# The column table of a graph layer turned during set-up, and 174 instead of 144 chunks taken from it

## The chip, the cores and the metric

The kernel runs on one core of one Trainium2 chip. The metric is the device time of one execution in microseconds; a profiled execution gives a span (first to last instruction) as well. Engines are called PE (matmul; its weight loads are PEld), DVE, ACT, POOL and SP, as in the profile.

## The reference, cut to what matters

There are 12500 nodes with 128 features and 200000 edges that are sorted by destination. Each node's normalised row is sent along its edges, the incoming rows are averaged, and a network of four layers with a residual ends it.

```python
h = jnp.maximum(_layernorm(x, axis=-1), 0.0)
# _L0_gnn_ref(z=h, edge_index=(src, dst)):
msgs = z[src]
agg = jax.ops.segment_sum(msgs, dst, num_segments=n)
deg = jax.ops.segment_sum(jnp.ones((src.shape[0],), z.dtype), dst, num_segments=n)
agg = agg / jnp.maximum(deg, 1.0)[:, None]
h = jax.nn.relu(agg @ Wg + z @ Ws + bg)
h = jnp.tanh(h @ W1 + b1)
h = jnp.tanh(h @ W2 + b2)
x = x + (h @ W3 + b3)
```

## The kernel before

**Chunks.** The edges are cut into 1563 chunks of 128. For each chunk the 128 source rows must stand in SBUF with one edge on each partition; PE then multiplies them with a one-hot matrix (`oh`, made by DVE for groups of 8 chunks, in 5 buffers) and adds the result into the sums of a block of up to 512 nodes, in PSUM (`agg`, and `edge` for chunks that lie across two blocks). Chunks are added in their order.

**Three sources of rows.** (1) 1339 chunks are gathered by POOL with one indirect DMA each from `htab`, the table of normalised rows in DRAM (tile `rows`, line 451 before). A gather writes into one of `AHEAD = 26` buffers, so POOL runs at most 26 gathers ahead of PE. (2) 80 chunks (10 groups of 8, "raw") are gathered from `x` during set-up, before `htab` exists; DVE normalises them later, group by group, in the main loop's first part (lines 266 to 280 on tile `raw`). (3) 144 chunks come from `tab`, the same table turned and kept in SBUF, with a node in each column. An edge's column is copied from `tab` at an index that a register holds. ACT makes 72 of these chunks (`column_copies`) and DVE 72 (`column_pairs`). One instruction handles two edges, so a chunk is 64 instructions, in 8 blocks with a register load (`TENSOR_LOAD places`) ahead of each. Then PE turns the finished 128x128 tile (`cols`) and ACT copies it to `turned`, which is used like `rows`. `SHARES` holds the two counts, `FROM` the first chunk that may be taken this way, `ENDS` the last for ACT and for DVE.

**Order.** PE, ACT, SP and the columns on DVE run in the order in which the code is written; the rest of DVE and the set-up are ordered by a scheduler. The main loop walks over the chunks and counts gathered chunks (`behind`). The column instructions of a chunk are written so that they end `MARGIN = 28` gathers before its use on ACT and 36 on DVE; the turn on PE is written 14 gathers before its use. ACT has 4 buffers of columns, DVE 6. The network's layers are spread between the chunks; from chunk `QUICK = 1312` a planner places them by its own reckoning of when each gather lands.

**Set-up.** The nodes are read in 11 pieces (of up to 10 tiles of 128 nodes). DVE and ACT normalise a piece into `h` (2 buffers), and SP writes it to `htab`. `indices` turns the edge lists on PE. POOL spends this time on the 80 raw gathers. In the main loop's first 48 chunks `own` reloads the rows of `htab` by SP in 25 pieces (`xb`, 256 KB each), and `own_turned` turns them on PE and copies them on ACT into `tab`. The columns wait for the whole of `tab`.

Of the kernel before, what the change touches and what calls it, by code (L numbers as in the profile page):

```python
# [22 lines left out]
F32 = mybir.dt.float32  # L23
# [8 lines left out]
P = 128  # L32
EPS = 1e-5
CPR = 16
BLK = 512
# [10 lines left out]
BEHIND = 2  # L46
EVERY = 4
AT = 3
SHARES = 72, 72
FROM, ENDS = 80, (1480, 1540)  # L50
MARGIN = 28
SUMS_AT, BANK = 1 << 25, 2048
AHEAD_OF_USE = 2
# [27 lines left out]
def windowed(ctx, tc, x, src, dst, Wg, Ws, bg, W1, b1, W2, b2, W3, b3, out, flag):  # L81
    nc = tc.nc
    N, D = x.shape
# [48 lines left out]
    for c in slots:  # L132
        shares = [n / k * (c < end) for n, k, end in zip(SHARES, within, ENDS)]
        owed = [o + n for o, n in zip(owed, [*shares, 1 - sum(shares)])]
# [6 lines left out]
    blocks, n = [], 0  # L141
# [46 lines left out]
    ps_m = ctx.enter_context(tc.tile_pool(name="ps_m", bufs=4, space=PSUM))  # L188
# [5 lines left out]
    for t, a in ((rsrc, src), (rdst, dst)):  # L194
        a = a[RAW0 * P : RAW1 * P].rearrange("(u e) -> u e", u=NRAW)[:, : GRP * P]
# [18 lines left out]
    for g in range(NRAW):  # L214
        t = raws.tile([P, GRP, D], F32, name=f"raw{g}")
# [7 lines left out]
    ident = const.tile([P, P], F32, name="ident")  # L223
# [14 lines left out]
    htab = dram.tile([NP, D], F32, name="htab")  # L238
    bytes_at = dram.tile([ahead_of + NROW * ROW + past_end], U8, name="bytes_at")
    tab = const.tile([P, NP], F32, name="tab")  # L240
# [24 lines left out]
    def centre(pool, xt, k, stats, bufs=2):  # L265
        nc.vector.tensor_reduce(stats[:, 0], xt, AX.X, ALU.add)
        nc.vector.scalar_tensor_tensor(xt, spread(stats[:, 0], k), -1.0 / D, xt, op0=ALU.mult, op1=ALU.add)  # L267
        sq = (pool.tile([P, PIECE, D], F32, name="sq") if bufs > 1 else pool.tile([P, GRP, W_RAW], F32, name="ohr", bufs=1)[:, :, :D])[:, :k]
        if bufs > 1:
            nc.scalar.activation(sq, xt, AF.Square)  # L270
        else:
            nc.vector.tensor_tensor(sq, xt, xt, op=ALU.mult)
        nc.vector.tensor_reduce(stats[:, 1], sq, AX.X, ALU.add)

    def factors(stats):
        nc.scalar.activation(stats[:, 1], stats[:, 1], AF.Sqrt, bias=eps, scale=1.0 / D)
        nc.vector.reciprocal(stats[:, 1], stats[:, 1])

    def scale(h, xt, k, stats):
        nc.vector.scalar_tensor_tensor(h, xt, 0.0, spread(stats[:, 1], k), op0=ALU.max, op1=ALU.mult)  # L280

    with tc.tile_pool(name="ln", bufs=2) as ln:
# [80 lines left out]
        for i, (t0, k) in enumerate(pieces):  # L363
            xt = ln.tile([P, PIECE, D], F32, name="xt", bufs=3)
            whole = min(N - t0 * P, k * P) // P
            rest = min(N - t0 * P, k * P) - whole * P
            if rest:
                nc.vector.memset(xt[:, whole, :], 0.0)
            nc.sync.dma_start(xt[:, :whole, :], x[t0 * P : (t0 + whole) * P, :].rearrange("(t p) d -> p t d", p=P))
            if rest:  # L370
                nc.sync.dma_start(xt[:rest, whole, :], x[(t0 + whole) * P : N, :])
            if i == 1:
                indices("src", src, 0, keep_src)
            stats = ps_a.tile([P, BLK], F32, name="agg")[:, : 2 * k].rearrange("p (s t) -> p s t", s=2)
            xt = xt[:, :k]
            centre(ln, xt, k, stats)
            factors(stats)
            h = ln.tile([P, PIECE, D], F32, name="h", bufs=2)
            scale(h[:, :k], xt, k, stats)
            nc.sync.dma_start(htab[t0 * P : (t0 + k) * P, :].rearrange("(t p) d -> p t d", p=P), h[:, :k])  # L380


        number = sp.tile([NROW, CPR], F32, name="number")
# [50 lines left out]
    ml = ctx.enter_context(tc.tile_pool(name="ml", bufs=2))  # L434
# [11 lines left out]
    def sp_dma(*a):  # L446
        tc.keep_in_program_order(nc.sync.dma_start(*a))
# [87 lines left out]
    def onehot(g):  # L535
        k = min(GRP, NCH - g * GRP)
        is_raw = raw(g * GRP)
        w = W_RAW if is_raw else W
        oh = ed.tile([P, GRP, W_RAW], F32, name="ohr", bufs=1) if is_raw else oh_bufs[g % OHS]
        newest[:] = [nc.vector.tensor_tensor(  # L540
            oh[:, :k, :w], lane[:, None, :w].to_broadcast([P, k, w]),
            dloc[:, g * GRP : g * GRP + k][:, :, None].to_broadcast([P, k, w]), op=ALU.is_equal,
        )]
        for c in range(g * GRP, g * GRP + k):
            if c in lanes[0] or c in lanes[1]:
                r, q = divmod(c, CPR)
                nc.vector.scalar_tensor_tensor(
                    oh[:, c % GRP, :W], lane[:, :W], partner[:, r, q // EVERY : q // EVERY + 1], oh[:, c % GRP, :W],
                    op0=ALU.is_equal, op1=ALU.subtract,
                )  # L550
        ohs[g] = oh
# [189 lines left out]
                s = out  # L741
            nc.vector.tensor_tensor(out, s, rd[:, a0 - n : a1 - n], op=ALU.mult)

    owns, xss, stores = {}, {}, []

    def own(s):

        n0 = s * BLK
        k = -(-min(BLK, N - n0) // P)
        hb = ml.tile([P, BLK // P, D], F32, name="xb")  # L750
        sp_dma(hb[:, :k], htab[n0 : n0 + k * P, :].rearrange("(t p) d -> p t d", p=P))
        owns[s] = hb

    def own_turned(s):

        k = -(-min(BLK, N - s * BLK) // P)
        hb = owns.pop(s)
        pt = ps_m.tile([P, BLK // P, P], F32, name="pm")
        for t in range(k):
            pe.transpose(pt[:, t, :], hb[:, t, :], ident)  # L760
        act.copy(tab[:, s * BLK : s * BLK + k * P], pt[:, :k, :].rearrange("p t n -> p (t n)"))

    def own_part(b):

# [155 lines left out]
            if w[1] is None:  # L920
                work.remove(w)

    nown = -(-N // BLK)
    own(0)
    own(1)
    own_turned(0)
    own(2)
    onehot(0)
    onehot(1)
    told_begins()  # L930
# [3 lines left out]
    for c in range(NCH):  # L934
        g = c // GRP
        at = c
        store(c - (SOON if c >= QUICK else LATE))
        if c % GRP == 0 and g + 2 < ngrp:
            onehot(g + 2)
            if raw((g + 2) * GRP):  # L940
                raw_scaled(((g + 2) * GRP - RAW0) // STEP)
            if g == 2 + NRAW + 2:
                worst = checked()
            if 2 <= g < 2 + NRAW:
                centre(ed, raw_rows[g - 2], GRP, raw_stats(g - 2), bufs=1)
            if g == 2 + NRAW + 5:
                factors(stats_raw)

        if c % (GRP // 2) == 0 and g + 2 < ngrp:
            copies, times = loading[1]  # L950
            while times and times[0] <= behind:
                times.pop(0)
                next(copies, 0)
        while c % GRP == GRP // 2 and counted < len(blocks) and reach[counted][-1] // GRP <= g + (c >= QUICK):
            count(counted)
            counted += 1
        while nxt < len(order) and nxt < behind + AHEAD:
            gather(order[nxt])
            nxt += 1
        if not raw(c) and c not in apart:  # L960
            behind += 1
            copies, times = loading[0]
            while times and times[0] <= behind:
                times.pop(0)
                next(copies, 0)
            while turns and turns[0][0] <= behind:
                turn(turns.pop(0)[1])
        if c >= QUICK:

            there = 7.5 + 1.251 * (NRAW * GRP + order.index(c)) if c not in apart else 0  # L970
            if c == QUICK:
                now = there - SPREAD
            while soonest() and max(now, soonest()[2]) < there:
                go_on(soonest())
            now = max(now, there) + 0.27
        add(c)

        lead = LEAD if c < QUICK else 2
        if done < len(blocks) and (c - lead if across[done] else c) >= reach[done][-1]:
            quick = reach[done][-1] + LEAD >= QUICK  # L980

            prev, older = (i if i >= 0 and reach[i][-1] + LEAD < QUICK else None for i in (done - 1, done - 2))
            older = None if quick and prev is None else older
            work.append([layers(done, prev, older), 0, 0, 0, quick and blocks[done][1] <= P])
            done += 1

        if c % TILE_EVERY == 1 and c // TILE_EVERY < NT:
            tallied(c // TILE_EVERY)
            if c // TILE_EVERY == NT - 1:
                outside(worst)  # L990
            if c // TILE_EVERY + EARLY < NT:
                seen(c // TILE_EVERY + EARLY)
        if c % 2 == 1 and c // 2 + 1 < nown:
            own_turned(c // 2 + 1)
            if c // 2 + 3 < nown:
                own(c // 2 + 3)
        if c < QUICK:
            if c % 2 == 0:
                go_on(work[0] if work else None)
                fetch_ahead(c)  # L1000
        if c == QUICK:
            for b, (_, n) in enumerate(blocks):
                if n < BLK:
                    own_part(b)
# [376 lines left out]
```

## Time and profile before

| | |
|---|---|
| runs | 1799.81, 1805.12, 1805.02 us; median 1805.02 |
| the profiled execution | 1800.16 us, with a span of 1798.4 us |
| busy PE / DVE / ACT / POOL | 1399.2 / 1034.4 / 1534.3 / 1348.5 us |
| mean granted PE clock | 0.83 |
| gathers of rows | 1339, the first issued at 107.3 us and the last at 1781.8 us |

Time is read from the engine that never waits for another: the share of busy time alone does not tell it, since an engine's gaps can be its own overhead. In the rows of a view, "x" is a count, and the text in brackets gives the idle time ahead of a row and what ended it. DVE, ACT and PE rows with a count are merged neighbours. [...]

### The profile page before, as it was taken

Reading aid. Unit: us, or ns where it says so; the run is one execution under the profiler, and the core shown is the slowest. Engines: PE = TensorE matmul, PEld = TensorE weight load, DVE = VectorE, ACT = ScalarE, POOL = GpSimd, SP = SyncE. Lnnn points to the kernel's source line nnn. Section 1 sums busy time; section 2 is a strip of 40 time slices with the busy share of each in tenths; the row PEclk is TensorE's granted clock in tenths of the full one; section 3 lists DMA queues with packets and bytes.
Section 4 is the critical chain, followed back from the end, with each engine's and each line's share of the span. In section 5 each row is a group of like instructions: output and inputs, shape, how many; then the busy total and the mean of one; then the engine's idle time right before and its main releaser. Section 6 shows DMA issues by size and latency. Waiting matters only on the chain.

```text
span 1798.4 us, 26668 instructions
## 1 busy us (share of the span) xinstructions
PE 1399.2 (78%) x5410; PEld 926.5 (52%) x5410; DVE 1034.4 (58%) x5580; ACT 1534.3 (85%) x5169; POOL 1348.5 (75%) x1428
## 2 busy tenths in 40 slices
PE   0047576878787888897888888787888888779998
PEld 0036454555455555555555555545555554555567
DVE  7965866666655656566565665556556655435400
ACT  1213999999999999999999999999999999998223
POOL 7777777777777777777777777777777777777774
PEclk9999999767887786877867868879787788778998
DMA  8954222222222222222222222222222222222221
GB/s 209 242 140 139 55 67 58 64 61 70 58 73 71 59 73 71 57 73 71 71 59 71 71 59 71 71 59 73 71 59 71 71 56 73 71 65 71 59 62 45
DMA packets 129832, 138.77 MB, mean 77 GB/s; under 512 B 30119, under 2 KB 106019, under 8 KB 129464
## 3 DMA queue, kind: packets, MB, share of 16 engines
q0 software_dynamic: 45408, 93.09, 19.9%
q1 hardware_dynamic: 80974, 40.37, 8.3%
q10 hardware_dynamic: 3276, 3.51, 0.7%
q14 instruction: 128, 1.05, 0.2%
q8 instruction: 46, 0.75, 0.2%
HBM read 123.84 MB, written 13.03 MB: 76 GB/s over the span
## 4 chain that ended last, share of the span: by engine, by line
ACT 29%; PE 25%; DMA 19%; issue 13%; POOL 9%; ACTq 4%; DVE 0%; DVEq 0%; POOLq 0%
ACT cols L518 25%; DMA rows<-htab,scol 19%; PE pm L441 17%; PE agg L441 6%; POOL rows L451 4%; POOL raw L217 4%; ACTq L461 4%; ACT h L518 3%; PE edge L441 2%; PE pm L444 1%; ACT turned L518 0%; ACT rd L521 0%; ACT o L521 0%; DVE cols L500 0%; DMA raw<-in_x_dram,rsrc 0%
## 5 line engine op out<-in xcount | busy, mean ns | idle before, releaser
L451 POOL DMA_INDIRECT rows<-htab,scol x1339 | 1267.8, 947 | 408.0 <-issue 226.7
L518 ACT ACTIVATE cols<-both_first,tab 128x2 f32<-128x2 f32 x4608 | 1351.2, 470 | 3.8 <-issue 1.9
L441 PE MATMUL pm<-h,w 128*128 128x512 f32 (+4 forms) x1344 | 795.0, 692 | 25.0 <-ACT h L518 20.5
L500 DVE SCALAR_TENSOR_TENSOR cols<-first_only,tab 128x2 f32<-128x2 f32 x4608 | 666.6, 218 | 250.4 <-issue 249.3
L441 PEld LDWEIGHTS agg<-oh,rows 128*128 128x128 f32 x1928 | 394.6, 253 | 426.8 <-DMA rows<-htab,scol 260.5
L441 PE MATMUL agg<-oh,rows 128*128 128x24 f32 x1928 | 398.7, 307 | 177.2 <-DMA rows<-htab,scol 172.2
L540 DVE TENSOR_TENSOR oh<-shared,dloc 128x192 f32<-128x192 f32 x186 | 65.5, 354 | 356.6 <-PE agg L441 211.0
L441 PEld LDWEIGHTS pm<-h,w 128*128 128x128 f32 x1344 | 243.6, 229 | 33.5 <-ACT h L518 22.4
L441 PEld LDWEIGHTS edge<-oh,rows 128*128 128x128 f32 x750 | 144.0, 233 | 164.8 <-DMA rows<-htab,scol 89.4
L441 PE MATMUL edge<-oh,rows 128*128 128x24 f32 x750 | 145.9, 289 | 63.3 <-DMA rows<-htab,scol 59.4
L518 ACT ACTIVATE h<-pm,b2c 128x512 f32<-128x512 f32 (+4 forms) x112 | 76.9, 689 | 51.6 <-PE pm L441 51.6
L217 POOL DMA_INDIRECT raw<-in_x_dram,rsrc x80 | 79.8, 998 | 25.6 <-issue 23.8
L587 DVE TENSOR_SCALAR_CACHE_REDUCE nearby<-nearby,parity 128x656 uint8<-128x656 uint8 x98 | 86.8, 886 | 0.0
L518 ACT ACTIVATE h<-pm,b1c 128x512 f32<-128x512 f32 (+4 forms) x112 | 76.6, 694 | 11.8 <-PE pm L441 11.2
L521 ACT COPY tab<-pm 128x512 f32<-128x512 f32 (+1 forms) x25 | 14.4, 577 | 68.1 <-PE pm L444 68.1
L340 PE MATMUL pm<-ident,idx_f 98*128 98x98 f32 x32 | 5.7, 373 | 82.5 <-DVE idx_f L334 54.4
L441 PEld LDWEIGHTS agg<-oh,turned 128*128 128x128 f32 x196 | 45.1, 258 | 36.6 <-issue 33.0
L444 PE MATMUL pm<-ident,cols 128*128 128x128 f32 x144 | 49.2, 342 | 10.7 <-ACT h L518 5.4
L518 ACT ACTIVATE turned<-pm 128x128 f32<-128x128 f32 x144 | 50.3, 349 | 7.4 <-PE pm L444 7.4
L740 DVE TENSOR_TENSOR mT<-agg,sums 128x136 f32<-128x136 f32 (+6 forms) x57 | 15.3, 272 | 71.3 <-PE agg L441 61.9
L441 PE MATMUL pm<-ident,h 128*128 128x128 f32 (+1 forms) x196 | 43.8, 309 | 14.4 <-ACT h L518 14.3
L270 ACT ACTIVATE sq<-xt 128x1280 f32<-128x1280 f32 (+3 forms) x11 | 12.7, 1153 | 44.6 <-DVE xt L267 35.4
(129 smaller groups left out, 850.8 us busy)
## 6 DMA issues: line engine op xcount, KB each, us to landing
rows<-htab,scol POOLq DMA_INDIRECT x1339
nearby<-bytes_at SPq DMA_DIRECT2D x98, 82.0 KB
xb<-htab SPq DMA_DIRECT2D x24, 256.0 KB
xb<-in_x_dram SPq DMA_DIRECT2D x23, 256.0 KB
out_dram<-o SPq DMA_DIRECT2D x23, 256.0 KB
xt<-in_x_dram SPq DMA_DIRECT2D x8, 640.0 KB
htab<-h SPq DMA_DIRECT2D x8, 640.0 KB
raw<-in_x_dram,rsrc POOLq DMA_INDIRECT x80
```

The lines of the kernel that those rows point to most:

```text
L217: nc.gpsimd.indirect_dma_start(out=t[:, j, :], out_offset=None, in_=x, in_offset=bass.IndirectOffsetOnAxis(ap=rsrc[:, g, j : j + 1], axis=0),)
L270: nc.scalar.activation(sq, xt, AF.Square)
L441: tc.keep_in_program_order(nc.tensor.matmul(*a, **k))
L444: tc.keep_in_program_order(nc.tensor.transpose(*a, **k))
L451: nc.gpsimd.indirect_dma_start(out=r, out_offset=None, in_=htab, in_offset=bass.IndirectOffsetOnAxis(ap=scol[:, c : c + 1], axis=0),)
L461: loads, vs = nc.values_load_multi_w_load_instructions(places[r : r + 1, q // EVERY, p0 : p0 + LOADS], engines=[kind], min_val=TAB_AT, max ...
L500: last[:] = [tc.keep_in_program_order(nc.vector.scalar_tensor_tensor(to, first_only, a, b.to_broadcast([P, 2]), op0=ALU.mult, op1=ALU.subtract
L518: tc.keep_in_program_order(nc.scalar.activation(*a, **k))
L521: tc.keep_in_program_order(nc.scalar.copy(*a))
L540: newest[:] = [nc.vector.tensor_tensor(oh[:, :k, :w], lane[:, None, :w].to_broadcast([P, k, w]), dloc[:, g * GRP : g * GRP + k][:, :, None ...
L587: done = nc.vector.tensor_scalar(w, w, parity[:, t % 2 : t % 2 + 1], None, op0=ALU.is_equal, op1=ALU.add, accum_out=found[:, t : t + 1])
L740: nc.vector.tensor_tensor(out, s, t, op=ALU.add)
```

## The change

In set-up, each piece `h` is now also turned on PE, four tiles at a time, and copied by ACT into `tab`. The reloads `own`, the turns `own_turned` and their places in the main loop are gone. Columns may be taken from chunk 30 on instead of 80, so that the column instructions are allowed from the first gather. ACT makes 75 chunks instead of 72, and DVE 99 instead of 72; so POOL gathers 1309 instead of 1339. ACT's first chunk is number 39 instead of 87 and its last 1471 as before; DVE's first is 35 instead of 95 and its last 1535 instead of 1531.

```diff
-SHARES = 72, 72
-FROM, ENDS = 80, (1480, 1540)
+SHARES = 75, 99
+FROM, ENDS = 30, (1480, 1540)
...
             nc.sync.dma_start(htab[t0 * P : (t0 + k) * P, :].rearrange("(t p) d -> p t d", p=P), h[:, :k])
+            for a in range(0, k, 4):
+                n = min(4, k - a)
+                p = ps_m.tile([P, 4, P], F32, name="pm")
+                for t in range(n):
+                    nc.tensor.transpose(p[:, t, :], h[:, a + t, :], ident)
+                nc.scalar.copy(tab[:, (t0 + a) * P : (t0 + a + n) * P], p[:, :n, :].rearrange("p t n -> p (t n)"))
...
-    def own(s):
...
-        sp_dma(hb[:, :k], htab[n0 : n0 + k * P, :].rearrange("(t p) d -> p t d", p=P))
...
-    def own_turned(s):
...
-            pe.transpose(pt[:, t, :], hb[:, t, :], ident)
-        act.copy(tab[:, s * BLK : s * BLK + k * P], pt[:, :k, :].rearrange("p t n -> p (t n)"))
...
-        if c % 2 == 1 and c // 2 + 1 < nown:
-            own_turned(c // 2 + 1)
-            if c // 2 + 3 < nown:
-                own(c // 2 + 3)
```

What this does to the order shows at three places. The first is ACT at the end of set-up and the beginning of the columns. `sq` is the square of a centred piece, `agg` its statistics, and the last piece is the one of 1024 columns. Before:

```order
L270 ACTIVATE sq<-xt 128x1280
L276 ACTIVATE agg<-agg,eps 128x10
L270 ACTIVATE sq<-xt 128x1024
L276 ACTIVATE agg<-agg,eps 128x8
L521 COPY tab<-pm 128x512 x24
L521 COPY tab<-pm 128x256
L461 TENSOR_LOAD places
L518 ACTIVATE cols_1157<-both_first,tab 128x2 x8
```

And now:

```order
L386 COPY tab<-pm 128x512 x2
L386 COPY tab<-pm 128x256
L276 ACTIVATE agg<-agg,eps 128x10
L386 COPY tab<-pm 128x512 x2
L386 COPY tab<-pm 128x256
L270 ACTIVATE sq<-xt 128x1024
L276 ACTIVATE agg<-agg,eps 128x8
L386 COPY tab<-pm 128x512 x2
L467 TENSOR_LOAD places
L524 ACTIVATE cols_1201<-both_first,tab 128x2 x8
```

The copies of two pieces stand ahead of the last piece's square, and the columns follow the last piece's copies at once.

The second place is DVE at the end of set-up. `oh_205` and the like are the one-hot matrices of whole groups, `ohr` and `degs` serve the count of edges, `raw_101` is the first raw group. Before:

```order
L540 TENSOR_TENSOR oh_205<-shared,dloc 128x192
L611 TENSOR_REDUCE ext<-dloc 128x1
L349 COPY partner<-pm 128x392
L557 SCALAR_TENSOR_TENSOR ohr<-firsts,shared 98x1568
L540 TENSOR_TENSOR oh_206<-shared,dloc 128x192
L562 TENSOR_REDUCE degs<-ohr 98x98
L540 TENSOR_TENSOR oh_207<-shared,dloc 128x192
L540 TENSOR_TENSOR oh_208<-shared,dloc 128x192
L612 TENSOR_REDUCE ext<-dloc 128x1
L266 TENSOR_REDUCE shared<-raw_101 128x8
```

And now:

```order
L546 TENSOR_TENSOR oh_205<-shared,dloc 128x192
L563 SCALAR_TENSOR_TENSOR ohr<-firsts,shared 98x1568
L546 TENSOR_TENSOR oh_206<-shared,dloc 128x192
L568 TENSOR_REDUCE degs<-ohr 98x98
L571 TENSOR_SCALAR begins<-pm 1x98
L467 TENSOR_LOAD places
L506 SCALAR_TENSOR_TENSOR cols_737<-first_only,tab 128x2 x8
```

A whole chunk of columns and half of a second one now stand ahead of `oh_207`, the matrices of chunks 24 to 31; the raw groups come after them, in turn with more columns. Before, the first columns on DVE came after six of the ten raw groups.

The third place is the head of PE's order. `idx_f` are the edge lists, `h` and `xb` the pieces of the table. Before:

```order
L340 MATMUL pm<-ident,idx_f 128x98 x32
L348 MATMUL pm<-ident,firsts_of 128x98 x4
L444 MATMUL pm<-ident,xb 128x128 x4
L441 MATMUL pm<-degs,ident_ones 1x98
L441 LDWEIGHTS zeros
L441 MATMUL agg<-zeros 128x512
```

And now:

```order
L385 MATMUL pm<-ident,h 128x128 x4
L340 MATMUL pm<-ident,idx_f 128x98 x16
L385 MATMUL pm<-ident,h 128x128 x94
L340 MATMUL pm<-ident,idx_f 128x98 x16
L348 MATMUL pm<-ident,firsts_of 128x98 x4
L447 MATMUL pm<-degs,ident_ones 1x98
L447 LDWEIGHTS zeros
L447 MATMUL agg<-zeros 128x512
```

All turns of the table stand in set-up, and the 16 turns of the destination list come after the last of them.

More of the change, by code (lines that the diff above doesn't have):

```diff
@@ L742, in merged @@
             nc.vector.tensor_tensor(out, s, rd[:, a0 - n : a1 - n], op=ALU.mult)
-    owns, xss, stores = {}, {}, []
-    def own(s):
-        n0 = s * BLK
-        k = -(-min(BLK, N - n0) // P)
-        hb = ml.tile([P, BLK // P, D], F32, name="xb")
-        sp_dma(hb[:, :k], htab[n0 : n0 + k * P, :].rearrange("(t p) d -> p t d", p=P))
-        owns[s] = hb
-    def own_turned(s):
[L756 to L759, printed above, removed]
-            pe.transpose(pt[:, t, :], hb[:, t, :], ident)
-        act.copy(tab[:, s * BLK : s * BLK + k * P], pt[:, :k, :].rearrange("p t n -> p (t n)"))
+    xss, stores = {}, []
     def own_part(b):
@@ L921, in go_on @@
                 work.remove(w)
[L923 to L927, printed above, removed]
     onehot(0)
```

## The prediction

> **What bounds the kernel now.** I read the view of the tile `rows` first, then the waits, then the order of time. The tile's view gives each gather's duration (least, median, most) and the first and last start; the waits give total, count and longest.
>
> ```profile
> L451 POOL DMA_INDIRECT rows<-htab,scol x1339: 940/944/1667, 107.3 to 1781.8; - x192
> ```
> ```profile
> POOL rows L451 <- issue: 226.7, 744, 0.3
> POOL rows L451 <- PE agg L441: 57.6, 189, 0.3
> ```
> ```profile
> 107.27 0.95 POOL L451 DMA_INDIRECT rows<-htab,scol  x1 [0.30 <-issue]
> ...
> 400.37 0.94 POOL L451 DMA_INDIRECT rows<-htab,scol  x1 [0.30 <-issue]
> 401.62 0.95 POOL L451 DMA_INDIRECT rows<-htab,scol  x1 [0.30 <-issue]
> ...
> 1781.76 0.94 POOL L451 DMA_INDIRECT rows<-htab,scol  x1 [0.30 <-issue]
> ```
>
> A gather takes 0.94 us and is followed by 0.30 us in which POOL issues the next; no wait is longer than 0.3 us, whatever it is put down to. So POOL gathers every 1.25 us from 107.27 to 1781.76 us, and nothing holds it up: 1338 steps in 1674.5 us. After the last one come 16.6 us of PE and ACT work up to the span's end, 1798.4 us. POOL's count of gathers is the bound, and the question is whether the other engines still keep up when it falls. Here is how full they are: busy time in three stretches (PE, PEld, DVE, ACT, POOL, then PE's clock).
>
> ```profile
> 180.00:240.00 60.00, 34.20 (x111) 26.28 (x112) 52.73 (x234) 60.00 (x217) 45.68 (x48) 1.00 0.21 55
> 1020.00:1080.00 60.00, 50.53 (x158) 30.33 (x157) 35.84 (x215) 60.00 (x210) 45.37 (x49) 0.69 0.26 68
> 240.00:1620.00 1380.00, 1143.89 (x4227) 733.34 (x4225) 802.53 (x4808) 1358.98 (x4670) 1043.32 (x1106) 0.79 0.26 67
> ```
>
> ACT is idle for 21.0 us of 1380. It never stops POOL, but it is as full as POOL.
>
> **Gathers.** 30 fewer, at 1.25 us: 37.5 us off POOL's row of gathers. The end follows if the last gather is still the one that the last block waits for.
>
> **Set-up.** Added are 98 turns, 29 copies and nothing on SP or POOL; removed from the main loop are 25 reloads, 98 turns and 25 copies.
>
> ```profile
> 71.01 1.48 DVE L280 SCALAR_TENSOR_TENSOR h<-xt,agg 128x1280 f32<-128x1280 f32 x1
> ...
> 77.54 1.48 DVE L280 SCALAR_TENSOR_TENSOR h<-xt,agg 128x1280 f32<-128x1280 f32 x1
> ...
> 85.37 2.85 PE L340 MATMUL pm<-ident,idx_f 98*128 98x98 f32 x16 [54.41 <-DVE idx_f L334]
> 91.17 1.21 DVE L280 SCALAR_TENSOR_TENSOR h<-xt,agg 128x1024 f32<-128x1024 f32 x1
> 96.00 5.12 SPq L447 DMA_DIRECT2D xb<-htab  x3
> 99.65 1.09 PE L444 MATMUL pm<-ident,xb 128*128 128x128 f32 x4 [6.03 <-DMA xb<-htab]
> 100.77 0.59 ACT L521 COPY tab<-pm 128x512 f32<-128x512 f32 x1 [10.42 <-PE pm L444]
> 109.85 0.62 PE L441 MATMUL agg<-oh,rows 128*128 128x24 f32 x2 [8.16 <-DMA rows<-htab,scol]
> ```
>
> A piece comes every 6.5 us. Its ten turns take 2.7 us (2.5 x 1.09) on PE, which stood idle here for 54 us, and its three copies 1.6 us on ACT. The copies of a piece now stand ahead of the square of a later one; with 2.7 + 0.6 us behind `h` they end before that square can start, except in the last piece, for which I allow 1 to 2 us. SP reads `htab` back at 96.00 us already, and the first gather is only due at 107.27, after the 80 raw ones. These 11 us hide it; a us beyond them would be a us of the end. The destination list's 16 turns wait for the last piece: 92.4 + 2.2 + 2.85 gives 97.4 us, the first matrices some 2 us later, needed at 109.85. So nothing is added, and `tab` is whole at about 97.5 us. The reloads had no waiter that mattered; without them SP's queue holds only `nearby` there.
>
> **ACT.** The tail of the old `tab` and the first columns, and a piece of the steady part:
>
> ```profile
> 172.56 0.37 ACT L521 COPY tab<-pm 128x256 f32<-128x256 f32 x1 [1.81 <-PE pm L444]
> 173.97 26.30 ACT L518 ACTIVATE cols<-both_first,tab 128x2 f32<-128x2 f32 x94 [1.03 <-DVE oh L547]
> ...
> 403.02 0.26 ACT L518 ACTIVATE turned<-pm 128x128 f32<-128x128 f32 x1
> 403.18 9.02 ACT L518 ACTIVATE cols<-both_first,tab 128x2 f32<-128x2 f32 x32
> ```
>
> A column instruction costs 26.30 / 94 = 0.280 us, a `turned` copy 0.16. Three more chunks are 3 x 64 x 0.280 = 53.8 us, 30 more turned tiles 4.8; and the time in which it all must be done is 37.5 us shorter: 96.1 us to find. The columns can start at 97.5 instead of 173.97 us, which gives 76.5, and the idle time gives 21.0: 97.5 us. It just fits, but some of the early start is lost, since ACT's row has `turned` copies in it and 4 buffers, so it can't run far ahead. I take it that ACT ends its columns without any lead and up to 15 us late. That costs nothing by itself: the turn stands 14 gathers (17.5 us) ahead of its use, and PE may lag POOL by 26 buffers, 32.5 us less the 2.6 us in which a row lands, so 30 us, before a gather waits. What the lost lead does at the end comes below.
>
> **DVE.** Groups first (busy, mean ns), then two blocks of columns.
>
> ```profile
> L587 DVE TENSOR_SCALAR_CACHE_REDUCE nearby<-nearby,parity 128x656 uint8<-128x656 uint8 x98 | 86.8, 886 | 0.0
> L540 DVE TENSOR_TENSOR oh<-shared,dloc 128x192 f32<-128x192 f32 x186 | 65.5, 354 | 356.6 <-PE agg L441 211.0
> L272 DVE TENSOR_TENSOR ohr<-raw 128x1024 f32<-128x1024 f32 x10 | 12.3, 1228 | 0.2
> ```
> ```profile
> 193.47 1.15 DVE L500 SCALAR_TENSOR_TENSOR cols<-first_only,tab 128x2 f32<-128x2 f32 x8
> 194.93 1.14 DVE L500 SCALAR_TENSOR_TENSOR cols<-first_only,tab 128x2 f32<-128x2 f32 x8 [0.31 <-issue]
> ```
>
> A block of 8 costs 1.46 us from start to start with its register load, a chunk 11.6. The 27 more cost 313 us, against 356.6 us in which DVE stood at `oh` because it was ahead of PE. Over the whole that fits. It does not where the raw groups are (chunks 24 to 104): 71 gathers now, 89 us, for 10 groups at four instructions of 1.23 (49 us), 10 matrices (4), six tallies (5) and 5.6 chunks of columns (65), so 123 us: 34 us are lost. The lead there: the matrices of chunk 24 are done at about 122 us (the first ones at 99.4, an estimated 5 us of small work, then one and a half chunks, 17.4) and needed at 107.3 + 24 x 1.25 + 2.6 = 140. So DVE comes at most 16 us late at the stretch's end, PE as much, and 30 us are free. It recovers later; cost nothing, bounds 0 and, if the lead were nil, 4 us.
>
> **The end.** Here PE does fall behind. The rows' own instructions on PE (two a chunk), PEld and POOL:
>
> ```profile
> 1500.00:1560.00 60.00, 14.32 (x88) 15.12 (x88) 45.38 (x49) 0.87 0.25 66
> 1560.00:1620.00 60.00, 14.43 (x80) 17.75 (x80) 45.38 (x49) 0.70 0.24 63
> 1620.00:1680.00 60.00, 17.20 (x105) 20.51 (x105) 45.38 (x49) 0.86 0.25 67
> 1680.00:1740.00 60.00, 16.52 (x112) 19.16 (x112) 45.37 (x49) 1.00 0.23 62
> ```
>
> POOL starts 48 gathers in each; PE adds 44, 40, 52 and 56. So it is 12 gathers (15 us) behind at 1620 and level again by 1740. All its waits from 1560 to 1700 us are these:
>
> ```profile
> PE pm L441 <- ACT h L518: 19.3, 6, 4.8
> ```
>
> It waits for ACT there, and ACT comes without its lead now. From chunk 1312 to 1540 there are 4 gathers fewer, 5 us less for the same layers. Together up to 20 us more lag, on 15: that grazes the 30 us. PE can make good what it made good before, 12 gathers in 120 us, then a little more up to the last gather. I take 3 us as left over at the end, between 0 (all made good) and 20 (nothing).
>
> **Sum.** The profiled execution's time is 1800.16 us, 1.8 over its span. 1800.2 - 37.5 + 3 = 1765.7. The median of the runs, 1805.02, lies 4.9 above it, with one run of three beside the profile; I add half, 2.4: 1768 us.
>
> **A rule against the change.** Long DVE instructions do hold a gather up:
>
> ```profile
> 103.70 1.20 DVE L272 TENSOR_TENSOR ohr<-raw 128x1024 f32<-128x1024 f32 x1
> ...
> 103.83 1.90 POOL L217 DMA_INDIRECT raw<-in_x_dram,rsrc  x1 [0.30 <-issue]
> ```
>
> This gather ended 0.8 us after the DVE instruction and took twice its 0.94. If the columns on DVE did the same, each of the 1728 more could cost up to its 0.14 us, 242 us. But POOL is as fast with 52.73 us of DVE work in a stretch (45.68) as with 35.84 (45.37). The Trainium skill's page "SBUF — State Buffer", section "SBUF: two separate sides", says that DVE and GpSimd share a pair of ports under an exclusive lock, which a DVE instruction with two SBUF inputs takes against a GpSimd one that reads SBUF. By that rule these columns, which have two such inputs, would hold gathers up too; the trace agrees for the long instruction, and for the columns it shows no cost.
>
> **The rivals.** First, the late stage: the lag of PE passes 30 us, gathers wait, and 10 to 20 us come back: 1775 to 1788. For it: the waits on ACT and the 95% of PE after them; against it: 16 us of room. Second, the early stage or set-up is worse than reckoned (lead nil on DVE, or the table late by more than 11 us): 5 to 15 us, 1773 to 1783. Third, ACT becomes the pace: if the early start gives under half of its 76.5 us, 40 us are missing, of which 30 are hidden by the buffers: 1778 or more. Fourth, slower: the gathers are stretched by the denser DVE columns. Its place is the whole main loop, its price 1389 gathers (with the raw ones) times the stretch, and it decides from 37.5 / 1389 = 27 ns a gather; at 50 ns the time is 1800 + 32 = 1837. Against it: 240 to 1620 us holds 1106 gathers of 0.943.
>
> **Chances.** Forecast 0.65 (its own range 1759 to 1774), late stage 0.15, early stage 0.08, ACT's pace 0.06, stretched gathers 0.06. The range runs from 1762.7, all made good and no half gap added, less 3 us for a few stretched gathers like the one above that may fall elsewhere (1759), to the late stage's end (1788). Within 0.3%, 5.4 us, the runs can't be told apart. Faster by more needs less than 1799.6: 0.65 + 0.15 + 0.08 + 0.02 of the third; the same 0.04; slower 0.06.
>
> **What would show it.** The changed profile should have 1309 gathers at 1.25 us from about 107 us; `tab` copies ending near 97 us; ACT near 100% busy from 100 to 1600; fewer waits of DVE at `oh`; PE late by up to 16 us around 240 us and by 20 to 30 near 1580. Waits of POOL over 0.3 us would say that the buffers ran out; a later first gather, that set-up grew.

## The result, and the profile after

The changed kernel takes 1816.03 us (median of 7 runs, 1809.53 to 1818.62) against 1804.84 for the kernel before in the same comparison: ratio 1.0059, interval 1.0042 to 1.0076. It is slower, where 1768 us were forecast. The profiled execution took 1811.47 us, with a span of 1809.7. The chain is the work that ended last, followed back from the end. Here it is on the page before, and then on the page after with the two largest groups of the changed kernel (busy, mean ns | idle ahead and what ended it):

```profile
ACT 29%; PE 25%; DMA 19%; issue 13%; POOL 9%; ACTq 4%; DVE 0%; DVEq 0%; POOLq 0%
```
```profile
ACT 58%; DVE 12%; PE 10%; ACTq 7%; issue 5%; DMA 5%; POOL 1%; DVEq 1%; SPq 0%; POOLq 0%
L457 POOL DMA_INDIRECT rows<-htab,scol x1309 | 1241.6, 948 | 434.9 <-issue 220.0
L524 ACT ACTIVATE cols<-both_first,tab 128x2 f32<-128x2 f32 x4800 | 1421.6, 522 | 7.0 <-issue 3.5
```

The 30 gathers are gone and one gather costs what it did, 948 ns (947 before). But ACT has 58% of the chain instead of 29%. Its busy time in the steady part (columns: span, then busy and count of PE, PEld, DVE, ACT, POOL), first before, then after:

```profile
600.00:900.00 300.00, 256.56 (x955) 165.10 (x954) 173.54 (x1023) 296.06 (x1016) 226.71 (x241) 0.76 0.26 68
```
```profile
600.00:900.00 300.00, 233.95 (x936) 153.65 (x941) 215.76 (x1341) 298.52 (x1033) 221.29 (x235) 0.80 0.25 65
```

ACT's share hardly differs. POOL's count does: 241 gathers in 300 us are its full pace of 1.249 us each; after the change it starts 235. It waits for buffers that PE has not emptied:

```profile
POOL rows L457 <- PE agg L447: 101.4, 259, 4.2
POOL rows L457 <- PE edge L447: 39.8, 92, 5.7
```

Each such row holds about 0.3 us that a gather always shows, so its sum is not what was lost. The gathers' starts tell that. From the first to the last of them stand 1675.2 us, 41.5 more than 1308 times 1.249; before it was 3.3 more. The spans differ by +11.3: -37.5 for 30 gathers, +38.2 of such stalls, +12.4 behind the last gather (29.0 instead of 16.6 us), -1.8 for an earlier first gather.

How late PE is, below called its lag (a gathered chunk has two weight loads on PE, 2678 for 1339 gathers before; the start of the second less the start of that chunk's gather, mean of the gathers within 15 us of the time named; at best 2.5 to 2.6 us), worked out from all rows of the gathers and of `agg` and `edge`:

| us | 150 | 200 | 300 | 600 | 900 | 1200 | 1500 | 1580 | 1650 | 1750 |
|---|---|---|---|---|---|---|---|---|---|---|
| before | 3.3 | 2.8 | 3.1 | 3.0 | 3.6 | 3.3 | 3.4 | 11.5 | 16.2 | 3.3 |
| after | 2.9 | 8.7 | 27.2 | 25.5 | 25.0 | 24.0 | 25.1 | 30.1 | 30.1 | 18.4 |

PE falls behind between 170 and 300 us and never catches up.

### The profile page after: what moved, and what is told of

Read it like the earlier page. It is cut to its first block, busy times and chain, and to the rows that moved or that the text cites. A ratio compares the mean times of both kernels' runs of the same rounds, so it can differ in the third digit from the quotient of the medians.

```text
span 1809.7 us, 28818 instructions
## 1 busy us (share of the span) xinstructions
PE 1319.6 (73%) x5418; PEld 903.1 (50%) x5440; DVE 1272.1 (70%) x7338; ACT 1591.0 (88%) x5395; POOL 1320.6 (73%) x1398
## 4 chain that ended last, share of the span: by engine, by line
ACT 58%; DVE 12%; PE 10%; ACTq 7%; issue 5%; DMA 5%; POOL 1%; DVEq 1%; SPq 0%; POOLq 0%
ACT cols L524 50%; ACTq L467 7%; PE pm L447 7%; DVE cols L506 7%; ACT h L524 5%; DMA rows<-htab,scol 3%; PE agg L447 2%; POOL rows L457 1%; DMA xt<-in_x_dram 1%; ACT turned L524 1%; DVEq L467 1%; DVE nearby L593 1%; DVE h L280 1%; DVE agg L266 1%; ACT rd L527 0%
## 5 line engine op out<-in xcount | busy, mean ns | idle before, releaser
L457 POOL DMA_INDIRECT rows<-htab,scol x1309 | 1241.6, 948 | 434.9 <-issue 220.0
L524 ACT ACTIVATE cols<-both_first,tab 128x2 f32<-128x2 f32 x4800 | 1421.6, 522 | 7.0 <-issue 3.5
L506 DVE SCALAR_TENSOR_TENSOR cols<-first_only,tab 128x2 f32<-128x2 f32 x6336 | 914.8, 217 | 303.7 <-issue 302.1
L447 PE MATMUL agg<-oh,rows 128*128 128x24 f32 x1884 | 349.7, 295 | 84.8 <-DVE oh L546 48.0
L447 PE MATMUL edge<-oh,rows 128*128 128x24 f32 x734 | 120.5, 266 | 22.2 <-DVE oh L546 16.1
L217 POOL DMA_INDIRECT raw<-in_x_dram,rsrc x80 | 78.1, 976 | 25.5 <-issue 23.8
L450 PEld LDWEIGHTS pm<-ident,cols 128*128 128x128 f32 x174 | 42.1, 242 | 90.7 <-ACT turned L524 48.9
L524 ACT ACTIVATE turned<-pm 128x128 f32<-128x128 f32 x174 | 69.8, 401 | 20.0 <-PE pm L450 20.0
L546 DVE TENSOR_TENSOR oh<-shared,dloc 128x192 f32<-128x192 f32 x186 | 64.5, 347 | 12.6 <-PE edge L447 10.6
L385 PE MATMUL pm<-ident,h 128*128 128x128 f32 x98 | 22.7, 412 | 68.3 <-DVE h L280 55.4
L447 PE MATMUL pm<-mT,wg 128*128 128x512 f32 (+4 forms) x56 | 33.7, 688 | 37.7 <-DVE mT L748 37.7
L447 PE MATMUL agg<-oh,turned 128*128 128x24 f32 x240 | 51.3, 296 | 4.9 <-ACT turned L524 4.2
```

What stands on the lines that cost most here:

```text
L217: nc.gpsimd.indirect_dma_start(out=t[:, j, :], out_offset=None, in_=x, in_offset=bass.IndirectOffsetOnAxis(ap=rsrc[:, g, j : j + 1], axis=0),)
L385: nc.tensor.transpose(p[:, t, :], h[:, a + t, :], ident)
L447: tc.keep_in_program_order(nc.tensor.matmul(*a, **k))
L450: tc.keep_in_program_order(nc.tensor.transpose(*a, **k))
L457: nc.gpsimd.indirect_dma_start(out=r, out_offset=None, in_=htab, in_offset=bass.IndirectOffsetOnAxis(ap=scol[:, c : c + 1], axis=0),)
L506: last[:] = [tc.keep_in_program_order(nc.vector.scalar_tensor_tensor(to, first_only, a, b.to_broadcast([P, 2]), op0=ALU.mult, op1=ALU.subtract
```

## The experiments

Edits are against the changed kernel. Two theories stood at first. A: the early stage does it; DVE has too much to do while it normalises the raw groups, PE waits for one-hot matrices, ACT stands in its fixed order behind PE, and the time lost there is never won back. B: ACT's 75 chunks are too many for the shorter run, whatever happens early. C, that DVE is the pace all along, was the third.

**Kernels on a chip with gaps.** Four edits (those of e11 to e14 below) ran first on two chips on which every kernel took 20% longer, the kernel before too (2162.92 and 2158.0 us). What was expected of them, on the first chip:

> The table is turned in set-up as in the changed kernel, but the shares and the first chunk are the old ones (72 and 72, from chunk 80; 1339 gathers). All theories but one expect the time of before within 0.3% (1800 to 1807): POOL gathers 1339 times at 1.25 us and nothing early is added to DVE. Only if the turning in set-up itself were the harm (PE, ACT or the scheduler's order there) would it be above 1810.

> The changed kernel, but DVE's columns may be used from chunk 136 only (after the raw groups), and are 92 instead of 99, so that DVE's density after chunk 136 is the same as in the changed kernel; ACT keeps its 75 from chunk 30. 1316 gathers. Theory A (DVE has too much to do while the raw groups are normalised; PE waits for its one-hot matrices, ACT in its fixed order stands for 38 us, and being full later it never makes that up): no lag of PE over 10 us before 300 us, ACT idle under 10 us there, 23 gathers less than before give 1771 to 1780. Theory B (75 chunks are too many for ACT in the shorter time, whatever the early stage): PE's lag reaches 25 to 30 us by the middle, gathers stall by 20 us or more, 1795 or more.

> The changed kernel with 70 instead of 75 chunks on ACT (5 x 64 column instructions of 0.28 us, 90 us of ACT's work, less); DVE's 99 and the early start stay. 1314 gathers. Theories A and B both have ACT as the pace after 300 us, so that PE's lag dissolves by about 1000 us, the gathers' stalls end there and the time is 1770 to 1782; A expects the lag of 20 to 30 us at 300 us to be there still, B expects none of it. If DVE were the pace all along (theory C), PE's lag and the stalls stay and the time is 1805 or more.

> The changed kernel with one ACT instruction written later: the square root over all raw groups' statistics, for which ACT stood 14.5 us at 286 us because DVE was late, now comes 7 groups of chunks later (still before its first use). Nothing is left out. If ACT is the pace from there on (A), the 14.5 us come back nearly whole: 1795 to 1802 against 1810 to 1816 of the changed kernel. If ACT's stop is only a symptom of a late DVE or PE (C), nothing changes: 1808 to 1818.

On the second:

> The kernel of e2 again, since the chip of e1 to e4 ran every kernel, the one before too, a fifth slower, with engines that stood between instructions. DVE's columns only from chunk 136, 92 of them; ACT's 75 from chunk 30; 1316 gathers. On a chip that runs the kernel before in 1800 to 1806: theory A (the early stage's load on DVE makes PE late and stops ACT for 38 us, which ACT, full later, never wins back) expects PE's lag under 10 us until 300 us and 1771 to 1780; theory B (75 chunks are too many for ACT in the shorter time in any case) expects the lag at 25 us or more by the middle and 1795 or more.

> The kernel of e3 again: 70 instead of 75 chunks on ACT, all else as in the changed kernel; 1314 gathers. A and B: ACT is the pace after 300 us, and 90 us less of its work let PE's lag dissolve by about 1000 us: 1770 to 1782; by A the lag at 300 us is still 20 to 30 us. By C (DVE the pace all along) stalls and lag stay: 1805 or more.

> The kernel of e4 again: only the one square root on ACT moved 7 groups later. A: ACT's stop of 14.5 us at 286 us goes and comes back nearly whole, 1795 to 1802. C: nothing changes, 1808 to 1818.

> The kernel of e1 again: the table turned in set-up, shares and first chunk as before. 1800 to 1807 by all theories, over 1810 only if the turning in set-up itself were the harm.

The ratios were 1.0174 (e1) and 1.0152 (e8) for the table alone, 1.0063 (e2) and 1.0103 (e5) with DVE later, 1.0251 (e3) and 1.0286 (e6) with 70 on ACT, 1.0170 (e4) and 1.0178 (e7) with the roots late, each to 0.004 to 0.007 either way. I leave them out of the argument: the traces there have gaps ahead of the instructions of all engines (last section), the changed kernel itself was not run there, and which engine sets the pace on such a chip stays open. All that follows is from chips on which the kernel before took 1802 to 1804 us.

**The two kernels again** (`e9_before_again`, `e10_after_again`, no edit).

> The kernel before, unchanged, once more with a profile. The chips of e1 to e8 ran it in 2158 to 2163 us instead of 1805, so a trace of it from such a chip is wanted. On such a chip: gathers still 1.25 us apart where nothing holds them, and the 350 us lost as gaps of a microsecond or so ahead of instructions of all engines. On a chip like the first: 1800 to 1806.

> The changed kernel, unchanged. On a chip like the first, 1810 to 1818 and a ratio of 1.006 to that before. On a chip like that of e1 to e8, the ratio is what the experiments there have to be compared with: theory A and B expect 1.01 to 1.03, since e4 and e7, which differ from it by one instruction's place, had 1.017 and 1.018.

Before: 1802.34 us (one run; the median of 12 more beside the changed kernel was 1803.96). After: 1810.54 us, ratio 1.0042 (1.0028 to 1.0057). The loss is there again, on another chip.

**DVE's columns only behind the raw groups** (`e11_dve_later`; 1316 gathers).

```diff
-SHARES = 75, 99
+SHARES = 75, 92
+FROMS = 30, 136
-    within = [sum(c < end for c in slots) for end in ENDS]
+    within = [sum(a <= c < end for c in slots) for a, end in zip(FROMS, ENDS)]
-        shares = [n / k * (c < end) for n, k, end in zip(SHARES, within, ENDS)]
+        shares = [n / k * (a <= c < end) for n, k, a, end in zip(SHARES, within, FROMS, ENDS)]
```

> DVE's columns only from chunk 136 (after the raw groups), 92 of them; ACT's 75 from chunk 30; 1316 gathers. On a chip that runs the kernel before in about 1804 us: theory A (the early stage's load on DVE makes PE late and stops ACT for 38 us, which ACT, full later, never wins back) expects PE's lag under 10 us until 300 us, ACT idle under 10 us there, and 1771 to 1780; theory B (75 chunks are too many for ACT in the shorter time in any case) expects the lag at 25 us or more by the middle and 1795 or more.

1799.91 us, 0.9983 (0.9973 to 0.9992). The early lag is gone (3.9 us at 300), and yet it builds up by itself: 8.0 at 600, 11.0 at 900, 21.7 at 1200, 28.4 at 1500. ACT from 600 to 900 us:

```profile
600.00:900.00 300.00, 236.12 (x977) 159.26 (x980) 216.00 (x1336) 300.00 (x1038) 226.84 (x241) 0.80 0.27 68
```

POOL is at full pace, ACT at 300 of 300, and PE drifts away: ACT has more to do than the gathers take. A alone is not enough: the time is the one that B named, but the lag came later than B had it (15.5 at 1000).

**Five chunks fewer on ACT** (`e12_act70`; 1314 gathers): `SHARES = 70, 99`.

> 70 instead of 75 chunks on ACT, all else as in the changed kernel; 1314 gathers. A and B: ACT is the pace after 300 us, and 90 us less of its work let PE's lag dissolve by about 1000 us: 1770 to 1782; by A the lag at 300 us is still 20 to 30 us. By C (DVE the pace all along) stalls and lag stay: 1805 or more.

1773.1 us, 0.9846 (0.9822 to 0.9871). The early lag is as large as after the change (27.1 at 300) but it dissolves: 18.1 at 600, 9.5 at 900, 3.7 at 1500. That is A's forecast. C falls: DVE does the same 99 chunks.

**A stop of ACT in the early stage taken away** (`e13_sqrt_late`): the square roots of the raw rows' variances, for which ACT stood 13.2 us at 288, are put seven groups of eight chunks later.

```diff
-        if g == 2 + NRAW + 5:
+        if g == 2 + NRAW + 12:
```

> The changed kernel with only the square root over the raw groups' statistics on ACT written 7 groups of chunks later. A: ACT's stop of 14.5 us at 286 us goes and comes back nearly whole, 1795 to 1802. C: nothing changes, 1808 to 1818.

1814.78 us, 1.0072 (1.0050 to 1.0095): nothing gained, which is a miss for A (C named this time, but e12 rules C out). The stop came back 28 us later at the next layer (row of e13's ACT, idle ahead in brackets):

```profile
329.19 0.69 ACT L524 ACTIVATE h<-pm,bgc 128x512 f32<-128x512 f32 x1 [13.58 <-PE pm L447]
```

PE is late, so ACT stands at whatever comes next; this place in its order is not what costs.

**The table from the set-up's pieces, with the old shares** (`e14_tab_only`): `SHARES = 72, 72`, `FROM = 80`.

> The table turned in set-up, shares and first chunk as before (72 and 72 from chunk 80, 1339 gathers). 1800 to 1807 by all theories, over 1810 only if the turning in set-up itself were the harm.

1803.76 us, 1.0001 (0.9992 to 1.0011). Turning the pieces in set-up costs nothing, and an early table gains nothing by itself. ACT made 118 columns, not quite two chunks; then the `turned` copy of the first stands in its order, and that waits for PE's turn, which is written 14 gathers ahead of the use:

```profile
124.83 9.85 ACT L524 ACTIVATE cols<-both_first,tab 128x2 f32<-128x2 f32 x35
202.37 0.28 ACT L524 ACTIVATE turned<-pm 128x128 f32<-128x128 f32 x1 [67.68 <-PE pm L450]
```

**What was still open** after these: is it ACT's count of chunks, or its work against the gathers' time; and does the early stage cost anything? The planner spreads ACT's chunks evenly over the places that are allowed. Counted in its lists, 3 of the 75 lie ahead of chunk 80, 9 up to 256, 57 from 256 to 1376 and 6 behind; of the 72 before, 0, 10, 56 and 6. So the three more are all early, and the early start pays for those alone. In the long middle ACT has one chunk more and POOL 18 gathers fewer. A sharper form of B: ACT's work between two chunks must fit into the gathers between them.

**DVE back at 72, ACT at 75** (`e15_act75_dve72`; 1336 gathers): `SHARES = 75, 72`.

> ACT keeps 75 chunks by pairs and DVE goes back to 72: 1336 gathers. The theory that ACT's work is measured against the time of the gathers: DVE's 27 chunks made the gathers of the steady part 1.9% shorter (66.80 to 65.52 us for 64 chunks, by the number of chunks that are gathered there), ACT's chunks there are as dense as before the change (57 of 1120 in both), so without DVE's 27 ACT is at 98 to 99% again, no lag builds up, and the time is before's less 3 gathers, 1795 to 1803 us. The rival, that 75 chunks are too many for ACT in themselves (58 us more work than before): the lag grows to the 30 us limit and the time is 1815 us or more. The rival that the early stage costs 20 us whatever ACT does: the early stage holds 11 us of columns of DVE fewer here, so a lag of 10 to 20 us at 300 us would show and dissolve slowly.

1799.13 us, 0.9982 (0.9972 to 0.9991). No lag until 1500 (3.0 at 300, 3.0 at 900, 4.6 at 1500). So 75 chunks on ACT are not too many in themselves.

**ACT at 72, DVE at 99** (`e16_act72`; 1312 gathers): `SHARES = 72, 99`.

> ACT 72 chunks, DVE 99: 1312 gathers. In the steady part ACT's work for 64 chunks falls by 0.114 chunks of 19.5 us, 2.2 us of 65.5, against the changed kernel. If ACT's rate against the gathers decides, it is just below full (98 to 99%): the early lag of 30 us dissolves slowly, is half gone at 1300 us, and the time lies between 1771 (all made good) and 1785. If only five chunks fewer or more help, because a threshold lies between 70 and 72, the time is 1795 or more.

1771.72 us, 0.9839 (0.9823 to 0.9856): three chunks fewer on ACT are worth some 40 us (1.0059 to 0.9839 of 1804). ACT and POOL in its middle:

```profile
600.00:900.00 300.00, 244.51 (x1004) 163.05 (x1003) 223.17 (x1388) 299.21 (x1030) 226.61 (x241) 0.80 0.26 68
```

ACT is just as full as after the change, but here it is catching up: the lag goes from 24.4 at 300 to 15.8 at 900 and 6.4 at 1500, and POOL hardly waits (its gathers take 5.8 us over their pace in all). This kernel and the one with 70 beat both others; the two can't be told apart.

**ACT at 70, DVE late** (`e17_act70_dve_later`; 1321 gathers): `SHARES = 70, 92` with `FROMS = 30, 136` as above.

> ACT 70 chunks, DVE 92, from chunk 136 on: 1321 gathers, 7 more than with 70 and 99. If the early stage costs nothing where ACT has room, since its lag of 29 us is made good by 925 us, the time is 8.7 us longer than with 70 and 99: 1779 to 1783. If the early lag costs 10 us or more even there, the time is the same as with 70 and 99 or shorter: 1773 or less. The lag at 300 us should be under 9 us in either case.

1782.84 us, 0.9895 (0.9878 to 0.9911): by the ratios 8.8 us slower than with 70 and 99, and its 7 gathers more make 8.7. Where ACT has room, an early lag of 27 us costs nothing.

**DVE at 105, ACT at 70** (`e18_act70_dve105`; 1308 gathers): `SHARES = 70, 105`.

> ACT 70 chunks, DVE 105: 1308 gathers, 6 fewer than with 70 and 99. In the steady part the gathers for 64 chunks take 65.52 us, 0.28 less, ACT's work stays: 96 to 97% of them. If ACT's rate decides and DVE has room (over 180 us of waits for PE and ACT at the end of a matrix with 70 and 99, of 70 us more work), it is 7.5 us faster than with 70 and 99: 1764 to 1768. If the early stage, where DVE has 4 us more work still, or DVE as a whole is at its limit, nothing is gained or time is lost: 1773 to 1785.

1794.9 us, 0.9950 (0.9932 to 0.9968): by the ratios 19 us are lost against 99. Here DVE has the largest part of the chain, 47% against 17% with 99 (chain of the page, then the longest wait of PE for DVE):

```profile
DVE 47%; ACT 15%; PE 14%; issue 13%; DVEq 5%; ACTq 2%; DMA 0%; POOL 0%; POOLq 0%
...
PEld pm L447 <- DVE mT L748: 108.9, 18, 11.8
```

I had put 180 us of waits of DVE down as room. They are no room: with 99 chunks, 139 us of them stand at `mT`, a layer's input, and that is what PE waits for next. That DVE is the bound here is read from this one trace.

**All of it in one table.** Time between PE's start on the first gathered chunk behind one number and behind another; the gathers between at 1.249 us; ACT's busy time in it, as the view by windows gives it. All from the rows of the profiled executions.

| chunks 264 to 1272 | gathers, us | ACT busy, us | time, us | lag at start, end |
|---|---|---|---|---|
| before (72, 72) | 1044.2 | 1037.5 | 1045.8 | 10.1, 11.7 |
| after (75, 99) | 1024.2 | 1039.6 | 1044.8 | 30.8, 29.0 |
| e11 (75, 92 late) | 1024.2 | 1041.8 | 1043.2 | 8.4, 27.4 |
| e15 (75, 72) | 1046.7 | 1034.8 | 1044.6 | 9.6, 7.7 |
| e16 (72, 99) | 1026.7 | 1005.3 | 1011.9 | 24.8, 10.3 |
| e12 (70, 99) | 1029.2 | 985.2 | 1011.2 | 26.6, 8.6 |
| e17 (70, 92 late) | 1027.9 | 986.2 | 1026.0 | 10.3, 8.3 |

ACT's work here is 1035 to 1042 us with 75 chunks and with before's 72 (51 or 52 of them lie in this stretch), and about 1005 with e16's (49). The 72 of before and of e16 differ in where they lie. After the change the gathers want 20 us less, and the stretch still takes ACT's time. In e11 these 20 us appear as 19 us of lag, since the buffers still have room at the start; after the change PE is 30 us late already, and they appear as stalls. From chunk 40 to 264 the time is 254.0 us before, 271.6 after, 251.8 in e11, 263.8 in e16, 266.6 in e12: with 99 chunks on DVE from chunk 30 the early stage takes 10 to 18 us longer than before, and where ACT has room PE then runs faster than the gathers and makes it good. In e15, where DVE starts as early with 72, it is 251.4.

## Why the prediction was wrong, point by point

**Gathers** held: 30 fewer at an unchanged 1.249 us wherever they did not wait. With the same 3 us for the end and 2.4 for the median, the sum gives 1771.9 us for e16's 1312 gathers, 1774.4 for e12's and 1783.1 for e17's, where 1771.72, 1773.1 and 1782.84 were measured. For e15's 1336 it gives 1801.9, and 1799.13 was measured. The working was right to 3 us for a kernel in which ACT keeps up; that three of the sums come within 1.3 us is partly luck, since 3 and 2.4 were rough allowances.

**Set-up** held: `tab` was complete at 98.2 us (97.5 forecast), and e14 shows no cost.

**ACT is the step that failed.** The sum of 96.1 us to find and 97.5 at hand was one account for the whole run. The need came out: ACT's busy time between its first and last columns rose from 1461.1 to 1518.4 us, 57 (53.8 and 4.8 forecast). The supply did not. ACT began at 101.6 instead of 174.0 us, 72 us earlier, but stood idle 43 us between that and 360 us. In e11, where PE is not late, it stood 33 us there, because it was ahead: two chunks were done, and the `turned` copy of the first waited for PE's turn:

```profile
129.89 6.24 ACT L525 ACTIVATE cols<-both_first,tab 128x2 f32<-128x2 f32 x22
141.29 0.28 ACT L525 ACTIVATE turned<-pm 128x128 f32<-128x128 f32 x1 [5.17 <-PE pm L451]
```

Time at the start can't be spent in the middle when the order lets ACT be two chunks ahead. The forecast saw that and took it as "some of the early start is lost"; it should have made the account stretch by stretch. In the long middle (chunks 264 to 1272) ACT had 1037.5 us of work for 1044.2 of gathers before, so some 7 us of room, and the change took 20 away. The third rival had the mechanism and its condition (under half of the early start) and got 0.06; its price, 1778 or more, still counted on the 30 us of buffers, which DVE's lateness had taken.

**DVE.** "At most 16 us late at the stretch's end" came out: PE's mean lag is 18.6 us for the 25 gathers from 235 us and 17.8 from 266, with the 2.6 us of the landing in it. The room at `oh` was used much as forecast: DVE's idle time there fell from 356.6 to 12.6 us, where 313 were to go. PE's wait from 110 to 300 us is the one forecast (first row: total, count, longest); that of the second row, from 240 to 340 us, was not:

```profile
PEld agg L447 <- DVE oh L546: 41.4, 6, 10.2
PEld pm L447 <- DVE mT L748: 13.7, 1, 13.7
```

"It recovers later; cost nothing" failed. At 315 us PE stands for the input of the first layer, which DVE makes behind more columns, and the lag goes from 18.5 to 33.6 us in one step (chunks 166 and 168). ACT stands behind PE in the meantime, the lag is 27 us at 300, and recovering needs room on ACT, of which there was none. The 30 us of buffers were given out twice, to DVE early and to ACT for the rest. By the ratios the change is 14 us slower than e11, with 7 gathers fewer (8.7): the early lag costs it some 22 us of the 48 between forecast and result, the middle and the end the rest.

**The end.** 3 us were forecast, bounds 0 to 20. The part behind the last gather grew by 12.4, with the lag at 30 us from 1580 to 1650, so the buffers were full as the first rival has it, but from 300 us on (5 to 8 us of stalls in each 300 us) and not from a late stage alone. In e11 it is that rival's late stage: 10.7 us of stalls between 1500 and 1650 us and none between 300 and 1500. In e16 the end takes 18.0 us, near before's 16.6.

**A rule against the change.** Gathers were not stretched by DVE's columns; the fourth rival can be dropped, 948 ns with 99 chunks on DVE as with 72. Its price was also added wrongly: 1800 + 32 is 1832. "Long DVE instructions do hold a gather up" was read from too few rows, for length is not what decides. This gather of the kernel before starts inside a DVE instruction of the same length, which also reads two tiles in SBUF, and is not held up:

```profile
121.67 1.22 DVE L267 SCALAR_TENSOR_TENSOR raw<-shared,raw 128x1024 f32<-128x1024 f32 x1
122.26 0.94 POOL L451 DMA_INDIRECT rows<-htab,scol  x1 [0.30 <-issue]
```

In the traces before and after, 39 gathers start inside such a SCALAR_TENSOR_TENSOR on `raw`, and none takes over 0.95 us; 21 start inside the TENSOR_TENSOR that the prediction shows, and 16 of them take over 1.0, up to 1.97. The columns are of the first kind, and like it have one input that is a repeated value. Whether the operation or that repeated input decides is not shown.

**Left open:** how the early loss of 17.6 us after the change (271.6 instead of 254.0 us from chunk 40 to 264) divides between DVE's lateness and ACT's waits behind it. e13 took one such wait away, and another took its place. That the lag at 300 us is as large with 70 chunks on ACT, and gone with DVE late, speaks for DVE.

## What to carry to other kernels

When a change takes work from the engine that sets the pace, set the new pace against the work of each other engine between the same two points of the program, and not against its idle time over the whole run: 7 us of room in 1044 were all ACT had. An early start is worth only what the written order and the buffers let an engine keep ahead. Moving three chunks back from ACT to the gathers turned a loss of 11 us into a gain of 29; cutting the fast engine too far moves the bound to the next (DVE, at 105 chunks).

## What the runs showed of the hardware

The chips of these runs differ in more than clock. Here is the same kernel (table early, old shares) on a chip with gaps (span 2194.4 us, granted clock 0.722) and on one without (1802.4 us, 0.831), groups of gathers and of ACT's columns:

```profile
L457 POOL DMA_INDIRECT rows<-htab,scol x1339 | 1267.0, 946 | 781.5 <-issue 299.8
L524 ACT ACTIVATE cols<-both_first,tab 128x2 f32<-128x2 f32 x4608 | 1345.9, 381 | 119.2 <-issue 113.1
```
```profile
L457 POOL DMA_INDIRECT rows<-htab,scol x1339 | 1269.0, 948 | 408.1 <-issue 259.9
L524 ACT ACTIVATE cols<-both_first,tab 128x2 f32<-128x2 f32 x4608 | 1344.5, 447 | 6.5 <-DVE dloc L404 3.9
```

The gathers take the same time, and ACT's columns keep it busy as long (1345.9 and 1344.5 us); what differs is the idle time ahead of them, 781.5 instead of 408.1 us and 119.2 instead of 6.5. PE and DVE stand longer too (in gaps over 0.15 us: PE 697.9 instead of 393.8 us, DVE 1121.2 instead of 746.4). Why the slow chips do so, the traces don't say.

The granted clock of PE, 0.830 before and 0.768 after, is no cause: of the changed kernel's own runs the fastest (1809.53 us) has 0.767 and the slowest (1818.62) 0.836. The kernel before shows 1.00 up to 318 us, but its first clock record lies there, and the matmuls of rows take 389 ns before and 388 after (median, 90 to 300 us).
